# First LSTM products of the last superchunk in one set, idle products, and earlier steps of the convolutions

## The chip, the cores and the metric

The kernel runs on one core of a Trainium2 chip. The metric is device time in microseconds, from one launch, median of several executions. The engines are named as in the profile: PE (TensorE, matmul), PEld (its weight loads), DVE (VectorE), ACT (ScalarE), POOL (GpSimd) and SP (SyncE, which issues most DMAs). Each engine works through its own queue in order, so the order in which the program emits instructions is part of the design.

## The reference

Four residual graph layers are applied to x of 128 batches, 64 tokens and 256 channels, all in float32. Each begins with a layer norm and a ReLU. Layer 0 is a graph convolution with two batch norms, layers 2 and 3 are attention. The change lies in layer 1, and in the parts of layers 0 and 2 that are woven into it:

```python
h = relu(einsum('ts,bsh->bth', adj, x @ Wg0 + bg0))
h = relu(einsum('ts,bsh->bth', adj, h @ Wg1 + bg1))
for p in range(1, 5):
    nw = T // p
    wins = h[:, :nw * p, :].reshape(B * nw, p, H)        # windows of p tokens
    last = lstm_last(Wih[p-1], Whh[p-1], bih[p-1], bhh[p-1], wins)
    h = h.at[:, arange(nw) * p + (p - 1), :].set(last)   # last token of each window
```

So four LSTMs run one after the other over the same h: for p = 1 every token is a window, for p = 4 each window has four tokens. Each LSTM rewrites the last token of each of its windows, and the next one reads the result. Gates are i, f, g, o.

## The kernel before

Tokens are handled in 16 chunks of 512 (8 batches of 64 tokens), and layer 1's LSTMs take two chunks at a time: 8 superchunks (`sc` 0 to 7). The tile `hT` holds the h of a superchunk, channels on partitions, in two halves k = 0, 1 of the channels; DVE writes new states into it (L729, L733).

`lstm` is a generator: between its parts it yields, and the caller puts steps of other streams there. The yields of the four LSTMs of a superchunk are numbered n = 0 to 21. For p = 1 there are two parts with two yields each (n = 0 to 3); p = 2 has n = 4 to 7, p = 3 has 8 to 13, p = 4 has 14 to 21. The first yield of an LSTM stands in the middle of its first products, the second after the x-products of step 1, the last after its last state.

The first products of an LSTM (L790) multiply the first token of every window by three gates' weights: 3 gates x 2 output halves c x 2 input halves k = 12 products. `sets` says over which windows: with one set, each product covers all windows (336 columns at p = 3, 256 at p = 4). In the last superchunk of the kernel before, p = 3 and p = 4 take p - 1 strided sets; some of those windows' first tokens are not written by the LSTM before, so their products do not depend on its last states. A strided set has 176 or 160 columns at p = 3, and 96 or 80 at p = 4. For p > 1 the k = 0 products come first in each set.

PSUM has banks with the tags y, z, x and ps, two of each. Gate i of the first products lies in y, g in z, o in x; a bank comes free when ACT has applied the gate's function to it (L769 for first products, L718 for later steps). Then the steps of the LSTM follow: `y<-xd`, `z<-xd` or `z<-hT` (x-products of the coming step), then `y<-hd` and others (products of the state); `xd` and `hd` are sums and differences made on POOL and DVE. POOL and DVE also make other sums, and L835 adds products into the gates on DVE.

The other streams, each a generator too:

- `convolutions(c)`: the graph convolutions of a coming chunk. Its steps in order: scale (L542), DVE transposes, a trip through DRAM and the load of x; `add_squares` (L276, residual); `ln_stats` (L165, L166 on DVE, then the root on POOL, L99 and L100); the scale and shift (DVE, L183) and two applies on ACT (L185); two more applies; aggregation on PE (L206, `agg_b`); copies; product v (L557); `bounded` (L563); product u (L571); `biased` (L577); aggregation (`agg_c`); and two steps that write hT.
- `residual(c)`: adds h to x. `ahead(c)`: layer 2's norm of a finished chunk; its two apply steps (L183, L185) and its DVE transposes (L264) come at the places of `LATE`, n = 1, 1 and 2, from superchunk 2 on.

The tuple `CONV` gives the n of each step for superchunks 1 to 6. Its first part is for the even chunk, whose first step already came at n = 20 of the superchunk before, so its entries begin with `add_squares`; its second part is for the odd chunk and begins with the first step. Superchunk 0 has its own tuple `FIRST`. At one n, residual steps come first, then convolutions, then `LATE`, then other steps of `ahead`. The order on PE, DVE, POOL and SP (and ACT) is exactly that of emission; nothing is reordered by a scheduler.

`keep_busy(n, name)` (L153) issues n transposes of the identity into a `ps` bank, which nothing reads. Before the change it is used near the start and ahead of the LSTMs.

Of the kernel before, what the change touches and what calls it, by code (L numbers as in the profile page):

```python
# [19 lines left out]
def kernel(  # L20
# [35 lines left out]
    NCH = B * T // CH  # L56
    SUP = 2
# [28 lines left out]
    def bank(name, tag="ps"):  # L86
        return psum[0][0].tile([P, CH], F32, tag=tag, name=name, bufs=psum[0][1][tag])
# [65 lines left out]
    def keep_busy(n, name):  # L153

        ps = bank(f"idle_{name}")
        for i in range(n):
            nc.tensor.transpose(ps[:, :P], ident, ident)
# [772 lines left out]
    def residual(c, hT):  # L930

        i = c % SUP
        mid = l1r.tile([P, Q, CH * KD // Q], F32, tag="g", name=f"hm_{c}", bufs=3)
        for k in range(KD):
            for e in range(2):
                nc.vector.transpose(
                    mid.rearrange("p (e h) (j k c) -> p k e j h c", e=2, j=NJ, k=KD)[:, k, e],
                    hT[:, k, :].rearrange("p (h t i j e) -> p i e j h t", h=Q // 2, i=SUP, j=NJ,
                                          e=2)[:, i, e])
        far = put(mid, f"h{c}")  # L940
        yield
        dst = hT[:, i, :].rearrange("p (q n) -> p q n", q=Q)
        get(dst, far)
        yield
        add_squares(xs[c], xs[c], dst)
        yield

    def lstms(sc, hT):
        hv = hT.rearrange("p k (t b) -> p k t b", t=T)
        for p in range(1, SKIP + 1):  # L950
            if p > 1:
                parts = [hv]
            elif sc:
                parts = [hv[:, :, i * T // 2 : (i + 1) * T // 2, :] for i in range(2)]
            else:
                parts = [hv[:, :, :, i * NB : (i + 1) * NB] for i in range(SUP)]
            nw = parts[0].shape[2] // p
            sets = [slice(0, nw)]
            if p == 2 and sc:
                sets = [slice(0, nw // 2), slice(nw // 2, nw)]  # L960
            elif p > 2 and sc == NCH // SUP - 1:

                sets = [slice(i, i + (nw - 1 - i) // (p - 1) * (p - 1) + 1, p - 1) for i in range(p - 1)]
            for i, part in enumerate(parts):
                yield from lstm(p, part, sets, f"{sc}_{p}_{i}")

    def new_hT(sc):

        hTs[sc] = l1r.tile([P, KD, SUP * CH], F32, tag="hT", name=f"hT_{sc}")
# [40 lines left out]
    def load2(c, hT):  # L1010

        get(hT, far2[c])
        st[c, "hT2"] = hT.rearrange("p a (k n) -> p k a n", k=KD)
# [3 lines left out]


    RESIDUAL = (0, 2, 3), (1, 3, 4)
    CONV = (1, 2, 3, 3, 4, 4, 5, 6, 7, 8, 9, 10, 10), (3, 6, 7, 8, 8, 11, 12, 13, 14, 15, 16, 17, 18, 20)  # L1020
    BEGUN = 20
    FIRST = (0, 2, 3, 4, 4, 5, 6, 7, 8, 9, 10, 11, 12, 12), (3, 6, 7, 8, 8, 13, 14, 15, 16, 17, 18, 19, 20, 20)
    AHEAD = (4, 5, 10, 12, 14, 18), (6, 7, 21)
    LATE = 1, 1, 2
    FINAL = (4, 5, 10, 12, 12, 14), (6, 7, 11, 14, 14, 16)
    START = (0, 1, 0, 0, 0, 1, 0, 1, 1, 0, 0, 1, 1, 0, 1)

# [16 lines left out]
    with tc.manual_schedule(engines={mybir.EngineType.PE, mybir.EngineType.DVE, mybir.EngineType.Pool,  # L1044
                                     mybir.EngineType.Activation, mybir.EngineType.SP}):
        last = NCH // SUP - 1
        for sc in range(last + 1):
            todo = {}

            def units(places, unit):  # L1050
                for n in places:
                    todo.setdefault(n, []).append(unit)

            if sc:
                for i in range(SUP):
                    units(RESIDUAL[i], residual((sc - 1) * SUP + i, hTs[sc - 1]))
            else:
                units([0], convs[1])
            if sc < last:
                for i in range(SUP):  # L1060
                    units((CONV if sc else FIRST)[i], convs[(sc + 1) * SUP + i])
                new_hT(sc + 1)
            if sc > 1:
                units(LATE, aheads[sc * SUP - 3])
            if sc:
                for i in range(SUP):
                    units((FINAL if sc == last else AHEAD)[i], aheads[(sc - 1) * SUP + i])
            if sc + 1 < last:
                units([BEGUN], convs[(sc + 2) * SUP])
            for n, _ in enumerate(lstms(sc, hTs[sc])):  # L1070
                for u in todo.pop(n, ()):
                    next(u)
                if sc == last and n == 8:

                    new_hT(sc + 1)
                    for c in range(SUP):
                        load2(c, hTs[sc + 1][:, c, :].rearrange("p (q n) -> p q n", q=Q))
            assert not todo
# [415 lines left out]
```

## Time and profile before

| | |
|---|---|
| Time, median of 3 | 1960.11 us (1959.21 to 1960.13) |
| Span of the profiled execution | 1957.6 us (1959.53 us as a run) |
| Mean granted PE clock | 0.995 |
| PE busy | 1924.5 us, 98% |
| PE, first products L790 with one set, 256 columns | 504 records, 113.2 us |
| the same, 96 and 80 columns | 24 and 48 records, 4.8 and 10.4 us |
| ACT, all of L769 | 240 instructions, 134.1 us |

A float32 product shows as two records, because it goes through PE in two passes. A row in order of time gives start, length, engine, line, operation, tiles and shape, how many are merged, and in brackets how long the engine was idle before it and which engine's work ended that. Matmuls overlap, so that the length of one is longer than the distance from one to the next. The clock is a share of full speed.

### The profile page before, as it was taken

What the parts mean: (1) busy time and instruction counts of PE and PEld (TensorE: products, weight loads), DVE (VectorE), ACT (ScalarE), POOL (GpSimd) and SP (SyncE); (2) the same over time, 40 slices, a digit from 0 to 9 for tenths busy, and PEclk for the clock granted to TensorE, in tenths of its full rate; (3) what the DMA queues carried; (4) which work ended last, traced back from release to release, by engine and by line L of the source; (5) the groups of instructions that cost most, each with busy time, mean ns of one, the idle gap of its engine ahead of it and who ended that gap; (6) DMA issues with size and microseconds to landing.
All of it is one profiled execution on the core that took longest, in us unless ns stands there. A gap on an engine that the chain in (4) does not pass through costs nothing.

```text
span 1957.6 us, 37918 instructions
## 1 busy us (share of the span) xinstructions
PE 1924.5 (98%) x14857; PEld 1443.4 (74%) x14857; DVE 1143.7 (58%) x3000; ACT 945.4 (48%) x2120; POOL 367.2 (19%) x525
## 2 busy tenths in 40 slices
PE   9999999999999999999999999999999999999998
PEld 5444456896897798789689779788978966666665
DVE  6644444556556656655755755665545466566675
ACT  5654434455455455455454545545555444333443
POOL 2104211111211211121121121113112111111121
PEclk9999999999999999999999999999999899999999
DMA  4216802126324522521632542452134144444432
GB/s 135 61 35 220 294 27 90 58 80 199 114 81 163 171 82 91 193 94 60 212 103 86 179 151 82 137 190 89 74 126 132 49 141 130 130 130 141 136 118 83
DMA packets 109057, 238.23 MB, mean 122 GB/s; under 512 B 11216, under 2 KB 73168, under 8 KB 108880
## 3 DMA queue, kind: packets, MB, share of 16 engines
q1 hardware_dynamic: 108128, 234.47, 36.3%
q8 instruction: 117, 1.92, 0.4%
q0 software_dynamic: 320, 1.05, 0.2%
q14 instruction: 60, 0.49, 0.1%
q10 hardware_dynamic: 432, 0.30, 0.0%
HBM read 168.93 MB, written 66.85 MB: 120 GB/s over the span
## 4 chain that ended last, share of the span: by engine, by line
PE 88%; DVE 6%; ACT 4%; issue 1%; POOL 1%; DMA 0%; DVEq 0%; SPq 0%; ACTq 0%; POOLq 0%
PE x L826 21%; PE g L790 15%; PE z L826 10%; PE v L1095 6%; PE z L369 6%; PE y L826 5%; PE p_q L1102 5%; PE z L352 5%; PE p_k L1102 3%; PE v L557 3%; PE u L571 2%; PE agg_b L206 1%; PE s L1269 1%; PE o L1316 1%; PE tr L1129 1%
## 5 line engine op out<-in xcount | busy, mean ns | idle before, releaser
L835 DVE TENSOR_TENSOR gates<-gates,x 128x128 f32<-128x128 f32 (+2 forms) x384 | 119.5, 322 | 355.3 <-PE x L826 353.4
L826 PE MATMUL x<-xd,wset 128*128 128x128 f32 (+2 forms) x1280 | 285.1, 311 | 0.3 <-DVE gates L835 0.2
L826 PE MATMUL x<-hd,wset 128*128 128x128 f32 (+2 forms) x1152 | 246.7, 303 | 0.0
L826 PEld LDWEIGHTS x<-xd,wset 128*128 128x128 f32 x1280 | 202.1, 190 | 17.4 <-DVE gates L835 3.5
L718 ACT ACTIVATE gates<-gates,bias 128x256 f32<-128x256 f32 (+4 forms) x384 | 170.4, 491 | 66.6 <-DVE gates L835 63.7
L790 PE MATMUL g<-hT,wset 128*128 128x256 f32 (+6 forms) x816 | 194.9, 398 | 5.0 <-ACT gates L718 4.3
L884 POOL TENSOR_TENSOR gates<-gates 128x512 f32<-128x512 f32 (+2 forms) x48 | 74.9, 1560 | 637.7 <-ACT gates L718 628.1
L826 PEld LDWEIGHTS x<-hd,wset 128*128 128x128 f32 x1152 | 185.1, 191 | 5.0
L790 PEld LDWEIGHTS g<-hT,wset 128*128 128x128 f32 x816 | 153.0, 201 | 46.3 <-issue 10.0
L769 ACT ACTIVATE gates<-g,bias 128x512 f32<-128x512 f32 (+2 forms) x240 | 134.1, 607 | 76.2 <-PE g L790 73.2
L790 PE MATMUL g<-hT,wih 128*128 128x512 f32 x384 | 166.4, 592 | 0.0
L826 PE MATMUL z<-hs,wset 128*128 128x128 f32 (+2 forms) x768 | 154.1, 303 | 0.0
L832 ACT COPY gates<-y 128x128 f32<-128x128 f32 (+2 forms) x192 | 54.2, 293 | 199.3 <-PE y L826 198.8
L790 PEld LDWEIGHTS g<-hT,wih 128*128 128x128 f32 x384 | 72.3, 190 | 87.7 <-issue 81.8
L826 PEld LDWEIGHTS z<-hs,wset 128*128 128x128 f32 x768 | 119.8, 191 | 3.3
L775 DVE TENSOR_TENSOR cell<-gates 128x512 f32<-128x512 f32 (+2 forms) x80 | 51.2, 663 | 115.6 <-ACT gates L769 115.5
L352 PE MATMUL z<-agg,w_sb 128*128 128x512 f32 x256 | 114.1, 598 | 1.5 <-DVE agg L337 1.5
L369 PE MATMUL z<-h,w_sb 128*128 128x512 f32 x256 | 110.2, 592 | 0.0
L835 DVE TENSOR_TENSOR gates<-gates,z 128x128 f32<-128x128 f32 (+2 forms) x384 | 104.7, 317 | 0.1
L832 ACT COPY gates<-x 128x128 f32<-128x128 f32 (+2 forms) x192 | 56.5, 295 | 94.0 <-PE x L826 93.1
L718 ACT ACTIVATE gates<-x,bias 128x128 f32<-128x128 f32 (+2 forms) x192 | 74.7, 389 | 50.9 <-PE x L826 48.0
L826 PE MATMUL z<-hT,wset 128*128 128x128 f32 (+1 forms) x512 | 97.5, 303 | 0.0
(210 smaller groups left out, 3540.6 us busy)
## 6 DMA issues: line engine op xcount, KB each, us to landing
wset<-wfar SPq DMA_DIRECT2D x96, 960.0 KB, 6.4
hT<-far_h SPq DMA_DIRECT2D x116, 128.0 KB, 3.0
far_h<-hm SPq DMA_DIRECT2D x16, 512.0 KB, 6.2
far_n<-xs SPq DMA_DIRECT2D x16, 512.0 KB, 6.6
xs<-far_n SPq DMA_DIRECT2D x64, 128.0 KB, 3.3
far_x<-xs SPq DMA_DIRECT2D x16, 512.0 KB, 2.6
x<-far_x SPq DMA_DIRECT2D x64, 128.0 KB, 3.4
xt<-in_x_dram SPq DMA_DIRECT2D x15, 512.0 KB, 4.0
```

The source lines that it names most:

```text
L352: nc.tensor.matmul(ps, w1_sb[:, k, m * P : (m + 1) * P], agg[:, k, :], start=(k == 0), stop=(k == KD - 1))
L369: nc.tensor.matmul(banks[c, m], w2_sb[:, k, m * P : (m + 1) * P], h1[c][:, k, :], start=(k == 0), stop=(k == KH - 1))
L557: nc.tensor.matmul(banks[m], wg0_sb[:, k, m * P : (m + 1) * P], agg[:, k, :], start=(k == 0), stop=(k == KD - 1))
L718: nc.scalar.activation(gate(q, c, part), src, AF.Tanh if q == 2 else AF.Sigmoid, bias=bs[:, q * KD + c : q * KD + c + 1])
L769: nc.scalar.activation(columns_of(gate(q, c)), natural(banks[q, c][:, :n].rearrange("p (w b) -> p w b", b=nb)), AF.Tanh if q == 2 else AF. ...
L790: nc.tensor.matmul(banks[q, c][:, :n].rearrange("p (w b) -> p w b", b=nb)[:, w, :], block(q, c, k), hv[:, k, w.start * p : (w.stop - 1) * ...
L826: nc.tensor.matmul(folded(self.psum(kind)), wsets[p, self.q][:, BLOCKS[kind][i], :], (ox[self.s] if part == "x" else oh)[kind], start=firs ...
L832: nc.scalar.copy(gate(self.q, kind // 5, halves[kind // 5]), self.psum(kind))
L835: nc.vector.tensor_add(gate(self.q, *dst), gate(self.q, *a), self.psum(kind))
L884: nc.gpsimd.tensor_mul(gates[:, 0, :, :n], gates[:, 0, :, :n], gates[:, 2, :, :n])
L1095: nc.tensor.matmul(ps[:, i, :], hT[:, k, j, :], w[:, k, first : first + D], start=(k == 0), stop=(k == KD - 1))
L1102: nc.tensor.matmul(ps.rearrange("p (a n) -> p a n", n=P), w[:, k, m * P : (m + 1) * P], hT[:, k], start=(k == 0), stop=(k == KD - 1))
```

## The change

Three edits. First, the strided sets of the last superchunk go: p = 3 and p = 4 there have one set, as elsewhere. Second, in the last superchunk 54 transposes that nobody reads are issued at five places: 4 after the x-products of p = 2 (n = 5), 18 at the end of p = 2 (n = 7), 10 after the x-products of p = 3 (n = 9), 14 at the end of p = 3 (n = 13), 8 after the x-products of p = 4 (n = 15). Third, in superchunks 1 to 6 the even chunk's statistics come at n = 1 in place of 2 and its first two applies at 2 in place of 3; the odd chunk's `add_squares` comes at n = 5 in place of 6, its statistics at 6 in place of 7 and its first two applies at 7 in place of 8.

```diff
@@ def lstms
             if p == 2 and sc:
                 sets = [slice(0, nw // 2), slice(nw // 2, nw)]
-            elif p > 2 and sc == NCH // SUP - 1:
-
-                sets = [slice(i, i + (nw - 1 - i) // (p - 1) * (p - 1) + 1, p - 1) for i in range(p - 1)]
@@
-    CONV = (1, 2, 3, 3, 4, 4, 5, 6, 7, 8, 9, 10, 10), (3, 6, 7, 8, 8, 11, 12, 13, 14, 15, 16, 17, 18, 20)
+    CONV = (1, 1, 2, 3, 4, 4, 5, 6, 7, 8, 9, 10, 10), (3, 5, 6, 7, 8, 11, 12, 13, 14, 15, 16, 17, 18, 20)
@@
+    IDLE = {5: 4, 7: 18, 9: 10, 13: 14, 15: 8}
@@ the loop over superchunks
                 for u in todo.pop(n, ()):
                     next(u)
+                if sc == last and n in IDLE:
+                    keep_busy(IDLE[n], f"l{n}")
```

## The prediction

> **What bounds the kernel now.** I read the page's first two parts and its chain, then the order of instructions on PE, ACT and DVE around the edited places, then stretches with their clock.
>
> ```profile
> PE 1924.5 (98%) x14857; PEld 1443.4 (74%) x14857; DVE 1143.7 (58%) x3000; ACT 945.4 (48%) x2120; POOL 367.2 (19%) x525
> PEclk9999999999999999999999999999999899999999
> PE 88%; DVE 6%; ACT 4%; issue 1%; POOL 1%; DMA 0%; DVEq 0%; SPq 0%; ACTq 0%; POOLq 0%
> ```
>
> PE is the bound: 98% busy, 88% of the chain. So only three things count: PE idle, PE work, PE clock. One slice of the clock row is an 8, and it lies where the last superchunk starts its p=4 LSTM. The stretches there (length, then PE, PEld, DVE, ACT and POOL busy, clock, DMA) and PE's order of time:
>
> ```profile
> 1510.00:1515.00 5.00, 5.00 (x34) 4.65 (x34) 2.61 (x9) 3.47 (x8) 1.17 (x1) 1.00 0.92 373
> 1515.00:1520.00 5.00, 3.08 (x19) 2.76 (x18) 4.05 (x13) 2.65 (x8) 1.33 (x4) 0.79 0.02 5
> 1520.00:1525.00 5.00, 5.00 (x25) 5.00 (x25) 0.46 (x2) 2.08 (x4) 2.12 (x5) 0.50 0.26 105
> 1525.00:1530.00 5.00, 5.00 (x26) 5.00 (x25) 0.00 (x0) 0.20 (x1) 0.00 (x0) 0.50 0.00 0
> ...
> 1517.21 0.46 PE L790 MATMUL g<-hT,wset 128*128 128x96 f32 x2 [1.26 <-ACT gates L718]
> 1518.33 13.51 PE L790 MATMUL g<-hT,wset 128*128 128x96 f32 x62 [0.66 <-ACT gates L718]
> 1531.63 1.14 PE L826 MATMUL y<-xd,wset 128*128 128x128 f32 x4
> 1534.27 0.96 PE L826 MATMUL y<-hd,wset 128*128 128x128 f32 x4
> ```
>
> PE looks fully busy from 1520 to 1530, but at clock 0.50: 31 narrow products (62 records, two passes each) take 13.3 us. The half clock runs from 1517.9 to 1535.0, 17.07 us. It starts after two waits in one place.
>
> In superchunk 2, at p=3:
>
> ```profile
> 674.97 6.94 PE L790 MATMUL g<-hT,wset 128*128 128x336 f32 x24
> 683.20 0.89 PE L826 MATMUL y<-xd,wset 128*128 128x168 f32 x4 [1.28 <-ACT gates L769]
> 686.77 0.84 PE L826 MATMUL y<-hd,wset 128*128 128x168 f32 x4 [0.17 <-DVE hd L671]
> 680.55 2.07 ACT L185 ACTIVATE cv<-xs,nmr_b,rstd_b 128x256 f32<-128x256 f32 x4 [4.59 <-DVE nmr_b L183]
> 682.53 1.80 ACT L769 ACTIVATE gates<-g,bias 128x336 f32<-128x336 f32 x4
> ```
>
> ACT stands idle 4.59 us for a scale that DVE delivers late, does four applies, and only then the first gates that free PE's banks. The same 1.28 to 1.29 us wait stands in superchunks 1 to 6.
>
> At p=1 to p=2 of superchunk 2 there is almost no wait, but little slack:
>
> ```profile
> 626.04 2.07 ACT L185 ACTIVATE h<-xs,nmr_n,rstd_n 128x256 f32<-128x256 f32 x4 [4.00 <-DVE nmr_n L183]
> 631.72 1.25 ACT L769 ACTIVATE gates<-g,bias 128x512 f32<-128x512 f32 x2
> 631.45 7.93 PE L790 MATMUL g<-hT,wset 128*128 128x256 f32 x36
> 639.35 1.94 PE L206 MATMUL agg_b<-adjt_bd,cv 64*64 64x64 f32 x64
> ```
>
> **The Trainium skill.** "TensorE: Matmul & The Clock Gate", Part 1, says that an activity monitor with a free-running window of 3413 ns halves PE's clock after an idle window and restores it after a busy one. The trace agrees on the halves and the window: 17.067 us is five of them. But the window before the drop was not idle; counting 256 columns as 0.216 us per pass, PE streamed about 35% of it. Windows at 42% (around 1474, p=3) kept the clock, and windows at 62 to 65% (the narrow products at half clock) did not restore it. Part 4 of that page says transposes do not count as activity. The trace disagrees: 15 idle transposes start in the 3.1 us from 2.7, 27 in the 2.8 us from 5.9, so transposes alone restored the clock. The page's "LDWEIGHTS" section ties the load to 128 columns whatever the matmul's width; here products of 96 columns start every 0.112 us per pass, just like transposes of 128. Narrowing below 128 saves nothing.
>
> **The change part by part** (times on the profiled span of 1957.6 us; that execution took 1959.53, the others 1959.21 to 1960.13, so a difference of spans is taken over to the median 1960.11).
>
> *Last superchunk, p=3.* Twenty-four products in two sets become 12 of 336 columns, 12 x 0.566 = 6.8 us. They wait for the first new hT (DVE L729, done 1473.78); 18 transposes, 18 x 0.112 = 2.0 us, sit in 1471.44 to 1473.45, inside that wait. Products end at 1480.65 (before: 1481.17). Six x-products (1.71) and ten transposes (1.12) follow, so the hd products start at 1483.5 and not 1484.06; hd itself is ready at about 1482.3. Gain 0.56. The four transposes at p=2 (0.45) fill the 0.33 us wait at 1449.75: nothing.
>
> *Last superchunk, p=4.* Thirty-six products become 12 of 256 columns at 0.4315. PE ends p=3 at 1514.92, 14 transposes reach 1516.48, and hT (L729 done 1516.76) releases the first six products; the last hT half is there at 1518.96, in time for the other six, which end at 1522.0. ACT is then late: four applies for the far stream wait for DVE until 1520.49 and end at 1522.5, and from the first gate to hd took 3.4 us before (1529.80 to 1533.19). So hd comes at 1526.0; six x-products and eight transposes fill 2.2 us of the gap. The hd products start at 1526.05 against 1534.27, gain 8.2, and the rest of the half clock (0.7 us) costs 0.36 no more. Sum for this superchunk: -9.1 us. The windows there are more than half filled, so I expect no new drop.
>
> *Odd convolutions, superchunks 1 to 6 (second tuple).* Adding moves to place 5, statistics to 6, the first half of the applies to 7. On DVE the add (1.28 us) goes into 649 to 655, where DVE waits for PE; its two loads (2.8 and 4.9 us to landing, issued by 646.8) should be in by 652. The statistics (2.14 us) go into DVE's idle 5.02 us before 667.47. No DMA is moved. The applies keep their place on ACT's queue, but their scale is ready at 676.7 and not 680.5, so they run inside the 4.59 us wait. Gates follow the products from 679.1; PE goes from the products' end, 674.97 + 6.80 = 681.77, through two (0.57) and four (1.14) x-products and the aggregation (1.09, its unhindered time at 479.34) to the hd products at 684.6 against 686.77. Gain 2.2, six times: -13.2.
>
> *Even convolutions (first tuple).* Statistics move from place 2 to 1, applies from 3 and 3 to 2 and 3. Here the move hurts. In superchunks 2 to 6 DVE's queue now has the 2.14 us of statistics ahead of the scale of the far stream (L183, at 625.85), so ACT's four applies at 626.04 start at 628.2, and behind them the gates of p=1's second part. Then two of this stream's applies (1.04) stand on ACT ahead of that part's last gates (L769 at 631.72). These start at 631.72 + 2.14 + 1.04 = 634.9 and free the first x bank at 635.6. PE's fifth product of p=2 needs that bank at 631.45 + 4 x 0.4315 = 633.18: a wait of 2.4 us, and 0.1 more for the sixth. Loss 2.55, five times: +12.7. In superchunk 1 no far stream is there: gates end at 472.6, before PE asks at 472.8: nothing. Given back: agg_b no longer waits for late applies, 1.87 us to 1.09, five times: -3.9.
>
> *Clock.* The new 2.4 us waits leave down to 30% of a window, under the 35% that dropped it before. About half of the positions of a window do so. With wide products behind the wait one window at half clock is enough, 3.4/2 = 1.7 us. None at all is the lower bound, five the upper (8.5); I take two, +3.4.
>
> Sum: -9.1 - 13.2 + 12.7 - 3.9 + 3.4 = -10.1, so 1950.
>
> **Rivals.** (a) The p=2 wait does not arise, because ACT gets there early enough: for it speaks that ACT is only 48% busy; against it, the queue order above. Then 12.7 and 3.4 fall away: 1934. (b) Slower: the clock. If each new wait drops the clock and holds it for three windows, five times 5.1 us stand in place of 3.4: +22, 1972. It decides from about 13.5 us of clock loss, 1.6 windows each time; against it, only narrow products held it down before. (c) The last superchunk keeps a drop at p=4 as its gaps are longer without the narrow sets, and gives 2 and not 9 us: 1957. (d) Early statistics on DVE do not help p=3, because a load lands late and the add blocks DVE: the 13.2 is gone, 1963.
>
> **How the numbers follow.** Forecast 0.64, its own range 1945 to 1955; (a) 0.12; (b) 0.08; (c) 0.10; (d) 0.06. The range 1941 to 1959 leaves out most of (a), all of (b) and (d). Within 0.2% is 3.9 us, about what this kernel's measurement can tell. Faster is the forecast, (a) and most of (c), 0.81; same 0.06, from (c) and the edges; slower 0.13.
>
> **What would show it.** A clock row with no 17 us of half clock at 1518; hd products of p=4 about 9 us sooner; no L185 before L769 at p=3 with a 4.59 us idle; a new PE wait of about 2.4 us on ACT L769 at the fifth product of p=2 in five superchunks and none in the first. Short half-clock records right after those waits are step five. I am wrong if those waits are absent, or if half-clock stretches there are many and long.

## The result, and the profile after

The changed kernel takes 1948.67 us (median of 4 executions, 1947.89 to 1950.89) against 1960.12 (1959.21 to 1960.85): a ratio of 0.9944, 95% interval 0.9926 to 0.9961, so 11.5 us faster. Its profiled execution is the longest of the four, 1950.89 us with a span of 1949.1; the span of before was 1957.6. The working below is made on spans, whose difference is 8.5 us.

The page of the kernel after, its busy times, clock row and chain:

```profile
PE 1918.5 (98%) x14839; PEld 1437.6 (74%) x14839; DVE 1143.4 (59%) x3000; ACT 947.3 (49%) x2120; POOL 367.8 (19%) x525
PEclk9999999999999999999999999999999999999999
PE 88%; DVE 4%; ACT 3%; DMA 2%; issue 1%; POOL 1%; SPq 0%; DVEq 0%; ACTq 0%; POOLq 0%
```

The 8 in the clock row is gone, and PE is as much the bound as it was. The same four stretches of the last superchunk as before the change (length; PE, PEld, DVE, ACT, POOL busy; clock; DMA):

```profile
1510.00:1515.00 5.00, 5.00 (x34) 4.64 (x33) 2.35 (x9) 3.21 (x8) 1.43 (x1) 1.00 0.92 369
1515.00:1520.00 5.00, 4.80 (x31) 4.22 (x30) 4.05 (x12) 2.92 (x8) 1.15 (x3) 1.00 0.03 11
1520.00:1525.00 5.00, 4.19 (x24) 3.47 (x23) 1.50 (x5) 4.12 (x10) 2.30 (x6) 1.00 0.26 105
1525.00:1530.00 5.00, 5.00 (x46) 4.81 (x45) 2.93 (x12) 1.91 (x8) 0.00 (x0) 1.00 0.01 2
```

The clock is 1.00 in all of them, and from 1525 to 1530 PE has 46 records where it had 26. Kernel after, PE in order of time, at p = 4 there:

```profile
1515.18 1.69 PE L157 MATMUL idle_l<-ident 128*128 128x128 f32 x14
1517.07 5.45 PE L790 MATMUL g<-hT,wset 128*128 128x256 f32 x24 [0.20 <-DVE hT L729]
1523.33 0.76 PE L826 MATMUL y<-xd,wset 128*128 128x128 f32 x4 [0.81 <-ACT gates L769]
1526.08 0.71 PE L826 MATMUL y<-hd,wset 128*128 128x128 f32 x4
```

The products with hd start at 1526.08, 10.90 us after the end of p = 3 at 1515.18. Before they did so 19.35 us after it (1514.92 to 1534.27): 8.45 us gained. The wait ahead of the first products is 0.20 us, not 1.26 and 0.66.

Superchunk 2 at p = 3, kernel after, first PE and then ACT:

```profile
676.02 6.95 PE L790 MATMUL g<-hT,wset 128*128 128x336 f32 x24
682.80 0.73 PE L826 MATMUL y<-xd,wset 128*128 128x168 f32 x4
685.70 0.84 PE L826 MATMUL y<-hd,wset 128*128 128x168 f32 x4
```

```profile
677.80 2.08 ACT L185 ACTIVATE cv<-xs,nmr_b,rstd_b 128x256 f32<-128x256 f32 x4 [0.57 <-DVE nmr_b L183]
680.24 2.17 ACT L769 ACTIVATE gates<-g,bias 128x336 f32<-128x336 f32 x4 [0.36 <-PE g L790]
```

The four applies now start 1.78 us after the first product, not 5.58, and the gates wait for PE and no longer for the applies. From the first product to the products with hd it takes 9.68 us, where it took 11.80. That holds in superchunks 1 to 6.

Superchunk 2 from p = 1 to p = 2, kernel after, PE, then ACT, then the one row of DVE that releases ACT. At p = 2 the first products of superchunks 1 to 7 cover the windows in two sets of 256 columns, twelve products each:

```profile
629.01 1.94 PE L790 MATMUL g<-hT,wset 128*128 128x256 f32 x8
633.22 8.03 PE L790 MATMUL g<-hT,wset 128*128 128x256 f32 x28 [2.27 <-ACT gates L769]
```

```profile
625.83 2.07 ACT L185 ACTIVATE h<-xs,nmr_n,rstd_n 128x256 f32<-128x256 f32 x4 [6.23 <-DVE nmr_n L183]
631.52 1.08 ACT L185 ACTIVATE cv<-xs,nmr_b,rstd_b 128x256 f32<-128x256 f32 x2
632.50 1.24 ACT L769 ACTIVATE gates<-g,bias 128x512 f32<-128x512 f32 x2
```

```profile
625.67 0.13 DVE L183 SCALAR_TENSOR_TENSOR nmr_n<-mv_n,rstd_n 128x4 f32<-128x4 f32 x1
```

Here the change costs time. PE stops after four products (eight records) until ACT has freed a bank. ACT was idle for 6.23 us where it had been idle for 4.00, because the scale for the far stream (`ahead`, layer 2's norm) was queued behind the convolution's statistics on DVE; then two applies of the convolution stand ahead of the last gates. The wait comes in superchunks 2 to 6 (633.22, 795.56, 956.18, 1116.76, 1279.02) and not in superchunk 1. In three of the five a half-clock record of 3.41 us follows, at 633.61, 1118.30 and 1278.72; such a record is called a drop below. Kernel after, the stretch before the first drop, and one at the wait at 956.18, which kept the clock:

```profile
630.20:633.61 3.41, 1.14 (x6) 0.60 (x4) 2.56 (x8) 3.23 (x6) 0.00 (x0) 1.00 0.15 55
954.46:957.87 3.41, 1.69 (x7) 1.31 (x8) 2.56 (x6) 3.23 (x7) 0.93 (x1) 1.00 0.51 167
```

The first stretch is the clock window that ends where the half clock begins; PE was busy for 1.14 of its 3.41 us, and in the windows before the other two drops for 1.54 and 1.44. At 956.18 the boundary fell inside the wait, and the idle time was split between two windows with 2.86 and 1.69 us busy. From the first product of p = 2 to agg_b, superchunks 2 to 6 took 7.90 to 7.92 us before. Now they take 10.60 where the clock held and 12.17, 12.28 and 11.98 with a drop: 2.69 us for the two causes together, and 1.4 to 1.7 more for each drop.

### The profile page after: what moved, and what is told of

Read it like the earlier page. It is cut to its first block, busy times and chain, and to the rows that moved or that the text cites. A ratio compares the mean times of both kernels' runs of the same rounds, so it can differ in the third digit from the quotient of the medians.

```text
span 1949.1 us, 37871 instructions
## 1 busy us (share of the span) xinstructions
PE 1918.5 (98%) x14839; PEld 1437.6 (74%) x14839; DVE 1143.4 (59%) x3000; ACT 947.3 (49%) x2120; POOL 367.8 (19%) x525
## 4 chain that ended last, share of the span: by engine, by line
PE 88%; DVE 4%; ACT 3%; DMA 2%; issue 1%; POOL 1%; SPq 0%; DVEq 0%; ACTq 0%; POOLq 0%
PE x L826 22%; PE g L790 13%; PE z L826 11%; PE y L826 6%; PE z L369 6%; PE v L1095 5%; PE p_q L1102 5%; PE z L352 5%; PE p_k L1102 3%; PE u L571 3%; PE v L557 3%; DMA far_y<-ym 1%; PE agg_c L206 1%; PE s L1269 1%; PE o L1316 1%
## 5 line engine op out<-in xcount | busy, mean ns | idle before, releaser
L790 PE MATMUL g<-hT,wset 128*128 128x256 f32 (+2 forms) x744 | 191.8, 415 | 12.5 <-ACT gates L769 11.4
L790 PEld LDWEIGHTS g<-hT,wset 128*128 128x128 f32 x744 | 142.8, 195 | 60.6 <-ACT gates L769 17.5
```

The source lines that it names most:

```text
L790: nc.tensor.matmul(banks[q, c][:, :n].rearrange("p (w b) -> p w b", b=nb)[:, w, :], block(q, c, k), hv[:, k, w.start * p : (w.stop - 1) * ...
```

## The experiments

Times are medians; kernels of one group share the runs of the kernel before (1960.73 us for the first four, 1959.68 for the next four, 1960.68 for the last three). My theory is that of the prediction: three separate effects (last superchunk, odd convolutions, even convolutions) that add up, the last one a loss. The rivals are that the gains overlap, that the even part does no harm, and that the transposes nobody reads carry the gain of the last superchunk.

**The three parts alone.** The first kernel, `e1_last_only`, is the changed one with the old places:

```diff
-    CONV = (1, 1, 2, 3, ...), (3, 5, 6, 7, 8, ...)
+    CONV = (1, 2, 3, 3, ...), (3, 6, 7, 8, 8, ...)
```

> Edits 1 and 2 alone (one set, idle products), the convolution places as before. Theory: 9 us faster (about 1951), no half-clock record at p=4 of the last superchunk, and the 1.28 us waits at p=3 of superchunks 1 to 6 stay. Rival 'the convolutions carry it': within 3 us of before.

It took 1950.55 us (1949.73 to 1951.06), ratio 0.9948 (0.9933 to 0.9963): 10.2 faster. From the first full-clock record (5 to 9 us after the start in all kernels here) to the last 10 us its clock is full, and the waits of 1.28 us at p = 3 are all there. The spans differ by 9.3 us, so the part of the last superchunk is worth what its own stretch shows.

`e2_odd_only` is the kernel before with the new second tuple:

```diff
-    CONV = (1, 2, 3, 3, ...), (3, 6, 7, 8, 8, ...)
+    CONV = (1, 2, 3, 3, ...), (3, 5, 6, 7, 8, ...)
```

> Only the odd chunk's tuple of CONV. Theory: 13 us faster (about 1947): the waits at p=3 vanish in six superchunks, about 2.2 us each; agg_b still waits for its applies; the 17 us of half clock in the last superchunk stay. Rival 'the add at n=5 blocks DVE until its load lands': under 5 us faster, or slower.

1948.7 us (1948.15 to 1949.19), ratio 0.9939 (0.9922 to 0.9956): 12.0 faster, with no wait at p = 3 in superchunks 1 to 6. The half clock of 17.07 us in the last superchunk is still there, as PE's order of time shows:

```profile
1507.10 13.34 PE L790 MATMUL g<-hT,wset 128*128 128x96 f32 x62 [0.66 <-ACT gates L718]
```

This execution has one more drop, at 1462.95, where p = 3 of the last superchunk waits 1.47 and 0.89 us among its strided sets:

```profile
1462.96 7.27 PE L790 MATMUL g<-hT,wset 128*128 128x176 f32 x38 [0.89 <-ACT gates L718]
```

The kernel before has the same two waits (1.47 and 0.88 us) and kept its clock there, and its 38 records took 5.62 us. From the end of p = 2 to the products with hd it is 14.15 against 12.62 us, so the drop cost 1.5.

`e3_even_only` is the kernel before with the new first tuple:

```diff
-    CONV = (1, 2, 3, 3, ...), (3, 6, 7, 8, 8, ...)
+    CONV = (1, 1, 2, 3, ...), (3, 6, 7, 8, 8, ...)
```

> Only the even chunk's tuple of CONV. Theory: a wait of about 2.3 us at the fifth product of p=2 in superchunks 2 to 6, 0.8 us given back each time at agg_b, and one-window half clock after some of the waits: 9 to 17 us slower (1969 to 1977), with the 17 us of half clock in the last superchunk as before. Rival 'even tuple harmless': within 2 us of before.

1974.44 us (1974.03 to 1974.84), ratio 1.007 (1.0055 to 1.0085): 13.7 slower than before. The wait of 2.27 us stands in five superchunks, and four of the five drop the clock for one window. By the parts, 5 x 2.69 = 13.45 for the two causes, 6.2 for the four drops and -3.9 for agg_b make 15.7; the spans differ by 15.0. The rival that this part does no harm is out.

The three differences of medians sum to -8.5 and the whole change gave -11.5; overlap of the gains would have gone the other way. The drops make the difference. On the profiled spans the three are -9.3, -10.8 and +15.0, which is -5.1, against -8.5 for the whole. The drop at p = 3 in `e2_odd_only` and the fourth drop in `e3_even_only`, which the changed kernel's execution does not have, are 3.1 of these 3.4 us. `e4_last_odd` leaves out the harmful part only:

```diff
-    CONV = (1, 1, 2, 3, ...), (3, 5, 6, 7, 8, ...)
+    CONV = (1, 2, 3, 3, ...), (3, 5, 6, 7, 8, ...)
```

> All edits but the even chunk's tuple. Theory: 22 us faster than before (about 1938), so 11 us faster than the changed kernel, no half-clock record between start and end; agg_b waits 0.8 us in superchunks 2 to 6. Rival 'gains overlap, the wait at p=2 is only PE arriving earlier at something else': about the changed kernel's time, 1948.

1936.88 us (1936.76 to 1937.3), ratio 0.9879 (0.9864 to 0.9894), 11.8 faster than the changed kernel, at full clock up to the last 10 us. PE in superchunk 2:

```profile
628.84 7.93 PE L790 MATMUL g<-hT,wset 128*128 128x256 f32 x36
636.74 1.94 PE L206 MATMUL agg_b<-adjt_bd,cv 64*64 64x64 f32 x64
```

The 36 records run through without a wait, and agg_b is slow again (1.94 us, where it takes 1.16 when its inputs are there).

**What carries the last superchunk: one set, or the transposes?** `e5_no_idle` is the changed kernel without the transposes, `e6_sets_idle` the kernel before with them (and its old tuples and strided sets):

```diff
-                if sc == last and n in IDLE:
-                    keep_busy(IDLE[n], f"l{n}")
```

> The changed kernel without its 54 idle products. Theory: PE stands idle 2.3 us at p=3 and 1.9 us at p=4 before the first products, and the stretch from the end of the p=4 products to its hd products has only 1.3 us of work in 4 us, so a window falls under about 40% and the clock drops there; with wide work behind it one or two windows: 1 to 5 us slower than the changed kernel (1950 to 1954). Rival 'idle products do not matter, one set is what counts': within 1 us, and no half clock in the last superchunk.

```diff
+    IDLE = {5: 4, 7: 18, 9: 10, 13: 14, 15: 8}
...
+                if sc == last and n in IDLE:
+                    keep_busy(IDLE[n], f"l{n}")
```

> The kernel before with the idle products added, narrow sets kept, convolution places as before. Theory: the idle products fill the wait at p=4, no drop of the clock there, so 36 narrow products take 8 us and not 16: 5 to 8 us faster than before (1952 to 1955), but slower than one set with idle products by 1 to 3 us. Rival 'narrow products themselves drop the clock': the half clock stays, within 2 us of before.

`e5_no_idle` took 1947.78 us (1946.56 to 1951.63), 0.994 (0.9925 to 0.9955). I had expected it slower than the changed kernel; it is not distinguishable from it by its median. Its four executions explain the spread: mean clocks of 1.0, 0.999, 0.997 and 1.0 go with 1946.56, 1948.87, 1951.63 and 1946.69 us. The profiled one had no drop before the last 10 us, although the gap is back in PE's order of time:

```profile
1511.26 5.45 PE L790 MATMUL g<-hT,wset 128*128 128x256 f32 x24 [1.73 <-DVE hT L729]
```

Yet the products with hd start 10.91 us after the end of p = 3, and in the changed kernel 10.90: the wait for hT is there with or without work to fill it. At p = 3 they start 11.04 us after the end of p = 2, and in the changed kernel, where the ten transposes stand on the path, 12.08. So in this execution one set alone gave the whole gain, as the rival had it.

`e6_sets_idle` took 1954.32 us (1953.97 to 1954.73), 0.997 (0.9959 to 0.9982): 5.4 faster than before by the transposes alone. The narrow products at p = 4, with the clock kept:

```profile
1518.03 7.15 PE L790 MATMUL g<-hT,wset 128*128 128x96 f32 x62 [0.63 <-ACT gates L718]
```

The same 62 records took 13.51 us before. From the end of p = 3 to the products with hd it is 12.93 us, 6.4 less than the 19.35 of before and 2.0 more than with one set; at p = 3, 0.6 more than with one set. So the half clock, and not the number of narrow products, made most of the loss, and either edit alone took it away. Between the medians of `e6_sets_idle` and `e1_last_only` lie 3.8 us where I had expected 1 to 3; 1.9 of the distance between these two kernels belongs to a wait outside the LSTMs, shown below with `e9_behind_no_idle`.

**Can the loss be avoided and the early applies kept?** `e7_stats_behind` emits the even chunk's statistics at n = 1 as the change does, but behind the two apply steps of the far stream:

```diff
+            if 1 < sc < last:
+                todo[1].append(todo[1].pop(2))
             for n, _ in enumerate(lstms(sc, hTs[sc])):
```

> The changed kernel, with the even chunk's statistics at n=1 emitted behind the far stream's two apply steps in superchunks 2 to 6. Theory: of the wait of 2.4 us at p=2 the 2.14 us part goes and at most 0.3 us is left (two applies, 1.04 us, less 0.8 us of slack); agg_b does not wait; no half-clock record: 14 us faster than the changed kernel (about 1935), 2 to 3 us faster than all edits without the even tuple. Rival 'the two applies ahead of the last gates make the wait': the wait stays above 1 us, within 6 us of the changed kernel.

1935.29 us (1935.09 to 1936.48), ratio 0.9875 (0.9858 to 0.9891): 13.4 faster than the changed kernel and 1.6 faster than `e4_last_odd`. PE in superchunk 2:

```profile
628.80 8.43 PE L790 MATMUL g<-hT,wset 128*128 128x256 f32 x36
637.17 1.16 PE L206 MATMUL agg_b<-adjt_bd,cv 64*64 64x64 f32 x64
```

The 2.27 us wait is gone and agg_b is fast: the order of two streams on DVE's queue was the larger part of the cause. The two applies ahead of ACT's last gates stayed, and they cost 8.43 - 7.93 = 0.5 us in each superchunk, where at most 0.3 was expected. `e8_applies_late` takes out the other half, the applies, and leaves the statistics where the change put them:

```diff
-    CONV = (1, 1, 2, 3, ...), (3, 5, 6, 7, 8, ...)
+    CONV = (1, 1, 3, 3, ...), (3, 5, 6, 7, 8, ...)
```

> The changed kernel with the even chunk's first applies back at n=3, its statistics still at n=1 ahead of the far stream's scale. Theory: the wait at p=2 falls by the two applies' 1.04 us, to about 1.3 us, too short to drop the clock: 8 to 11 us faster than the changed kernel (about 1939). Rival 'the statistics do nothing': no wait at p=2 left, 17 us faster (1932).

1941.82 us (1941.27 to 1942.22), ratio 0.9906 (0.9891 to 0.9921): 6.9 faster than the changed kernel. PE:

```profile
632.10 6.46 PE L790 MATMUL g<-hT,wset 128*128 128x256 f32 x28 [1.29 <-ACT gates L769]
```

The wait falls by 0.98 us, and five times that is 4.9. The spans differ by 9.6, and the rest is the three drops of the changed kernel's profiled execution (4.6), of which this one has none. I had expected 8 to 11 by medians, where the changed kernel's other executions had fewer drops.

From the first product of p = 2 to agg_b the loss against `e4_last_odd` is 1.71 us with the early statistics alone (`e8_applies_late`), 0.46 with the early applies alone (`e7_stats_behind`), and 2.69 with both. The two together cost more than their sum. That fits a slack of about 0.5 us ahead of the wait, which can be used up only once: what stands in the way for 2.14, 1.04 and 3.18 us costs 0.43, 0.58 and 0.49 less than that.

**The transposes once more, without other drops.** With the p = 2 waits gone the question of `e5_no_idle` can be put again. `e9_behind_no_idle` is `e7_stats_behind` without any transposes in the last superchunk; `e10_behind_less_idle` leaves out only the ten at n = 9, which stand on the path:

```diff
-    IDLE = {5: 4, 7: 18, 9: 10, 13: 14, 15: 8}
+    IDLE = {5: 4, 7: 18, 13: 14, 15: 8}
```

> The kernel with the statistics behind the far stream (e7), without any idle product. Theory (the idle products only guard the clock, and the ten at p=3 sit on the path): with the clock held, 1.1 us faster than e7 (about 1934.2), since the ten at n=9 no longer stand ahead of the hd products; gaps of 2.2 and 1.7 us come back, and executions whose window falls on one lose 1.7 us or more, so their spread is larger than e7's. Rival 'idle products are needed': slower than e7 by 1.7 us or more in most executions.

> e7 with the ten idle products at n=9 (p=3) taken out, the others kept. Theory: the hd products of p=3 start 1.1 us sooner and nothing else changes: 1934.2, spread as e7. Rival 'hd is late there too': no change, 1935.3.

`e9_behind_no_idle`: 1937.87 us (1937.26 to 1939.36), ratio 0.9887 (0.9871 to 0.9904), 2.6 slower than `e7_stats_behind` and `e10_behind_less_idle`. PE at p = 3, and the window ahead of its drop:

```profile
1459.34 8.74 PE L790 MATMUL g<-hT,wset 128*128 128x336 f32 x24 [2.24 <-DVE hT L729]
```

```profile
1456.50:1459.90 3.40, 1.16 (x5) 0.66 (x4) 2.56 (x5) 2.51 (x5) 0.47 (x1) 1.00 0.77 255
```

A half-clock record begins at 1459.93, and the same 24 records take 8.74 us instead of the 7.05 of `e10_behind_less_idle`. The drop costs 1.65 us: from the end of p = 2 to the products with hd it is 12.69 and not 11.04 us. At p = 4, with a gap of 1.73 us, the clock held, and the products with hd start 10.91 us after the end of p = 3. By its medians the rival that the transposes are needed has won. The profile does not bear that out, since most of the 2.6 us lies elsewhere, in the attention layers, 68 us after the LSTMs' last product:

```profile
1618.30 1.96 PE L1102 MATMUL p_q<-hT,w_sb 128*128 128x512 f32 x4 [1.67 <-DMA hT<-far_h]
```

PE waits there for a load. The wait is 1.26 us in `e5_no_idle` and 1.60 in `e6_sets_idle`, and none of the other ten profiles has it. From the last LSTM product to the end of the span these three take 385.7 to 386.2 us, the others 384.2 to 384.5. Their traces show a 16 KB packet of the instruction queue (q8) starting 63 to 64 us after the LSTMs' last product, while this load is under way; in the other ten no such packet starts between 55 and 68 us. These three also lie outside the others in their number of instructions (14785 and 14911 matmul records against 14829 to 14857). That the packet makes the load late, and that the number of instructions moves the packet, is not shown. So of the 2.8 us between the spans of `e9_behind_no_idle` and `e7_stats_behind`, 1.9 is this wait and 0.6 the last superchunk, the drop less the 1.04 us of the ten transposes that no longer stand on the path. What its other three executions, with mean clocks of 0.998 and 0.999, lost to the clock is not known.

`e10_behind_less_idle`: 1935.23 us (1934.87 to 1935.59), ratio 0.9872 (0.9858 to 0.9887), the same as `e7_stats_behind`. The stretch from the end of p = 2 to the products with hd is indeed shorter, 11.04 us (1457.75 to 1468.79) and not 12.08, but the profiled execution had a drop at 269.71, ahead of the LSTMs, where nothing was changed. The window before that drop:

```profile
266.30:269.70 3.40, 2.01 (x66) 1.44 (x66) 2.19 (x9) 2.18 (x4) 0.95 (x2) 1.00 0.00 0
```

Sixty-four of its 66 records are products of 64 columns. `e6_sets_idle` came through the same place without a drop. By the traces the ten transposes cost 1.04 us at their place, which the medians don't show.

`e11_behind_final` is `e10_behind_less_idle` with a step of the far stream in the last superchunk moved behind p = 4's first gates:

```diff
-    FINAL = (4, 5, 10, 12, 12, 14), (6, 7, 11, 14, 14, 16)
+    FINAL = (4, 5, 10, 12, 12, 14), (6, 7, 11, 15, 15, 16)
```

> e10 with the far stream's four applies of n=14 in the last superchunk at n=15, so that they stand behind the first gates of p=4 on ACT. Theory: these applies hold back the gates by 2 to 3 us; without them PE does not wait 0.8 us for bank y and hd comes before the x-products end: 1.5 to 2 us faster than e10 (about 1932.4). Rival 'the applies then hold up the copies of y behind them': within 0.5 us of e10.

1934.94 us (1934.46 to 1936.0), ratio 0.9872 (0.9857 to 0.9886): no gain, as its rival had it. The products with hd start sooner, 9.39 us after the end of p = 3 instead of 10.91, but PE then meets a new wait, since the applies now hold up ACT's copies of y:

```profile
1511.29 0.68 PE L826 MATMUL x<-xd,wset 128*128 128x128 f32 x4 [1.35 <-ACT gates L832]
```

From the first of these products to the last of the LSTM it is 40.28 us and no longer 38.80, so the 1.5 us are lost again.

The best versions, `e7_stats_behind`, `e10_behind_less_idle` and `e11_behind_final`, lie within 0.4 us of each other, some 13 us below the changed kernel and 25 below the one before.

## Why the prediction was right

The time (1948.67 against 1950) and the mechanisms hold. By its steps, on spans:

- *Last superchunk, p = 3.* Forecast 0.56. From the end of p = 2 to the products with hd it takes 12.08 us (1472.34 to 1484.42); before the change it took 12.62: 0.54.
- *Last superchunk, p = 4.* Forecast 8.2, and 8.45 was measured; with 0.36 for the rest of the half clock the superchunk gives 9.35 by the traces, and `e1_last_only` gives 9.3 by spans and 10.2 by medians. The forecast that no new drop comes held.
- *Odd convolutions.* Forecast 2.2 six times, and 2.12 was measured (11.80 less 9.68): 12.7 for 13.2. `e2_odd_only` gave 12.0 by medians.
- *Even convolutions.* Forecast 2.55 us lost five times and nothing in superchunk 1. Superchunk 1 lost nothing: from the first product of p = 2 to agg_b it takes 7.86 us before and after. In the others, where the clock held, this stretch is 2.69 us longer; the wait at the fifth product is 2.48 of it, from 629.01 + 4 x 0.4315 = 630.74 to 633.22. (The view counts 2.27, because it counts from the modelled end of the product before.) Both causes named are there: either alone costs less, 1.71 us the statistics on DVE and 0.46 the applies on ACT. The 0.78 us given back at agg_b is exact (963.66 - 962.57 = 1.09).
- *Clock.* Two drops of 1.7 us were assumed, three were in the profiled execution: 4.6 us and not 3.4. This is the term that was most mis-sized, though the estimate that about half of the positions of a window drop the clock fits: in the profiles of the changed kernel, `e3_even_only` and `e5_no_idle` 7 of 15 such waits did. The other three executions, with mean clocks of 0.998 to 0.999, had fewer, which is why the median is below the profiled one. How many drops come depends on where the windows lie, so that the median came out within 1.3 us of the forecast is in part luck.

The sum with the measured terms is -9.35 - 12.7 + 13.45 - 3.9 + 4.6 = -7.9, and the spans differ by 8.5. Of the 0.6 us left over, 0.3 lies ahead of p = 2 of superchunk 1 and 0.3 between p = 2 of superchunks 4 and 5; its cause was not looked for.

Of the rivals, (a), no wait at p = 2, did not arise; `e4_last_odd` and `e7_stats_behind` show what it would have given, 1937 and 1935, for its 1934. Rival (b) did not either, since each drop after a wait was over after one window. Nor did (c), or (d).

The prediction said of its clock reading that the half clock starts after two waits. It begins at 1517.92, inside the second one, so only the first 1.26 us and 0.25 of the second count. The prediction did not say which edit of the last superchunk does the work; it treated the transposes as filling for gaps. With one set the traces bear this out: at p = 4 it takes 10.91 us without transposes and 10.90 with them, and at p = 3 ten of them cost 1.04. With the strided sets kept they are worth 6.4 us at p = 4, because they hold the clock. What they guard against with one set is a drop at p = 3, which `e9_behind_no_idle` had in its profile (1.65 us) and `e5_no_idle` had not; how often it comes, two profiles can't tell.

## What to carry to other kernels

Before a step of a side stream is moved earlier, write down the queue of each engine that it passes: 2.1 us of statistics ahead of another stream's small scale cost more than the early applies gained, and swapping the two at the same place gave all of it back. Look at the clock in the stretch, not only at busy shares: a PE that is 100% busy at half clock hides a short wait ahead of it. When medians of near versions are compared, read the mean clock of each execution first, as a drop that comes in some of them is as large as what is measured. And compare the traces also far from the edit: in the profiles, most of the 2.6 us that seemed to be the worth of the transposes was a DMA wait in another layer.

## What the runs showed of the hardware

- The clock dropped after waits shorter than a window (3.413 us, the length of a single drop). The Trainium skill, "TensorE: Matmul & The Clock Gate", section "Why this matters for your kernels", asks for no gaps of PE above about 3 us. Here gaps of 2.27 us and 2.24 us dropped it, and before the change 1.26 and 0.25 us in one window of narrow products did; the measurement decides. What counted is how a gap lies in the window, which starts at another place in each execution: three of five equal waits dropped the clock in the profile after, four of five in that of `e3_even_only`, and none of the five in that of `e5_no_idle`. The waits of 1.47 and 0.88 us at p = 3 of the last superchunk kept the clock in the kernel before, where a window ended inside the first of them, and dropped it in `e2_odd_only`, where both lay in one window.
- One drop cost 1.4 to 1.7 us where products of 160 columns or more followed, and the clock was back after one window. In `e5_no_idle` the executions at clock 0.997 and 1.0 differ by 5.1 us, as three such drops would make. Narrower products are another matter: 96 and 80 columns kept the clock at half for five windows before the change, in `e2_odd_only` and in `e3_even_only`, yet in `e6_sets_idle` they ran at full clock once transposes had held it. One execution of the kernel before, of 1952.83 us, had a mean clock of 1.0 and was 7.9 us below the median.
- Busy time of PE is a poor measure of what the clock follows. The window ahead of the half clock in the kernel before was busy for 1.91 of 3.42 us and the one of 64-column products in `e10_behind_less_idle` for 2.01 of 3.40; both dropped. One of wide products with 1.69 of 3.41 did not. Columns streamed do better (my working over all thirteen profiles, from 9 us after the start to the last 10: 256 columns as 0.216 us per pass, and the 64-column products, which start four at a time within 0.02 us, four as one). The 13 windows ahead of a drop were filled to 0.19 to 0.38, and every full-clock window filled to 0.41 or more kept the clock. Two others, at 0.36 and 0.38, kept it too.
